# A graph layer with steps of six turns, gathers listed in pairs 20 chunks ahead, and another first part

## The chip, the cores and the metric

The kernel runs on one core of a Trainium2 chip. A core has five engines that run their own instruction lists in order and meet only through semaphores: PE (TensorE, matrix products, writes to PSUM), DVE (VectorE), ACT (ScalarE), POOL (GpSimd, which here issues the indirect DMAs) and SP (SyncE, which issues most other DMAs). The profile splits PE into PE (matmuls) and PEld (loading the stationary operand). The metric is device time in microseconds (us) of one execution; the figure given for a kernel is the median of several.

## What is computed

There are 12500 nodes with 128 features, and 400000 edges sorted by destination. Each edge carries one of two types.

```
def _L0_gnn_ref(X, edge_index, edge_types, W_data, b_data, W_control, b_control, W_self, b_self):
    src, dst = (edge_index[0], edge_index[1])
    Xs = X[src]
    m_data = Xs @ W_data.T + b_data
    m_ctrl = Xs @ W_control.T + b_control
    msg = jnp.where((edge_types == 0)[:, None], m_data, m_ctrl)
    agg = jax.ops.segment_sum(msg, dst, num_segments=X.shape[0])
    out = agg + (X @ W_self.T + b_self)
    return jax.nn.relu(out)
...
x = _layernorm(x + _L0_gnn_ref(x, edge_index, edge_type_2, ...), axis=-1)
```

Because the product with a weight is linear, the kernel sums the source rows of each destination and type first and multiplies the sums by the weights afterwards.

## The kernel before

**Tiles.** The edges form 3125 chunks of 128. A group (`g`, 25 of them) has 125 chunks and four windows (`i`); so there are 100 pairs `w = 4 g + i`, each with two windows: one of 11 or 12 chunks whose rows are fetched by indirect DMA ("gathered"), and one of 20 chunks whose rows are taken out of SBUF by one-hot matmuls ("picked"). Each row of x is held as three bf16 parts (`x3` in SBUF, `rows3` in DRAM), 384 numbers in all.

**Gathered window (`gathered`, L690 to L716).** For each chunk POOL issues one indirect DMA (L700) of 128 rows into a tile `msg`. PE then makes three matmuls with a one-hot matrix `psel` (L658) and one for the count (L712), all added up in a PSUM tile `sums`. After the last chunk DVE adds `sums` into the group's accumulator (`accumulate`, L682). The pool of `msg` has AHEAD = 24 buffers of one chunk each, and a gather stands in the program where its chunk is used. The framework's scheduler draws it forward on POOL's list as far as free buffers allow.

**Picked window (`picked`, L718 to L795).** The edges are first sorted into 100 cells of up to 32 slots by source block (`give_slots`, L505). This runs two pairs ahead, in small pieces: `before` (four matmuls, L537), `ranks` (DVE), `rank_matrix` (DVE, makes `rv`), `over`; then `put` (20 matmuls with `rv`, L601), `spread` (a copy by ACT, and two DMAs on SP: out to DRAM, L611, and back to all partitions as `pick`, L613), `turn_codes` (L621) and `keep_codes` (L631, L496, L498 on ACT, ending in `idx`). Edges beyond a cell's 32 slots go to a spare chunk that POOL gathers with `idx` (`spare_rows`, L747, tile `last`).

A picked window runs in `turns + 1` = 7 units, spread evenly over the pair:

- Units 0 to 5 each pick the rows of four cell columns: 16 matmuls (L732) into two PSUM tiles `got` (the pool `psg` has two), and two copies by ACT to `emsg` (L743).
- Units 1 to 5 also make the counts (L761) and sums (L658, with `esel`) of the unit before.
- Units 0, 1 and 3 let DVE make the one-hot `esel` (`choose`, L463). Unit 1 also issues the spare gather.
- Unit 5 carries `put` and `spread` for pair w + 2 and the last picks (`last_rows`).
- Unit 6 has no picks: it makes the sums of unit 5 and of the spare chunk, then `turn_codes` and `keep_codes`, then the addition by DVE.

**The order of the work.** `merged` sorts the units of all streams of one pair by a position between 0 and 1 and writes them out in that order: the chunks of a gathered window two pairs back (LAG = 2), the picked units, the slot pieces (0.1 to 0.75 for `begin`, 0.6 for the pick matrix), the index work of the next group (`prep_e` in the second pair of a group, `prep_p` in the third), and the parts of the finished group (`finish`). The scheduler moves instructions only where its own estimate finds an engine waiting. On each engine the list is in order, so what stands behind a waiting instruction waits too.

**The first part (L199 to L380, L903 to L918).** SP loads the first destinations of all windows into one tile `first_i`, the first groups, `near_i`. ACT issues four loads of x (L241) and then the weights (L274, L275). DVE makes tables, the windows' places (`place_i`, L372) and `near`. Then the slots of pairs 0 and 1 are made while x is split into three parts (`split_x`, L229), and `store_rows` writes the parts to DRAM. Gathers can start once they are there.

Of the kernel before, what the change touches and what calls it, by code (L numbers as in the profile page):

```python
# [46 lines left out]
AHEAD = 24  # L47
# [101 lines left out]
def short_path(ctx, tc, const, ident, eps, wT, brow, bad, x, src, dst, etype, ws, bs, out):  # L149
# [49 lines left out]
    first_i = keep.tile([1, NG, NWIN], I32, name="first_i")  # L199

    def load_first(kind):
        for i, (k, _, c, _) in enumerate(windows(0)):
            if k == kind:
                nc.sync.dma_start(
                    out=first_i[:, :, i:i + 1],
                    in_=dst.rearrange("(o g e) -> o g e", o=1, g=NG)[:, :, c * P:c * P + 1],
                )
# [65 lines left out]
    for i, (w, b) in enumerate(zip(ws, bs)):  # L273
        nc.scalar.dma_start(out=wn[:, i, :], in_=w)  # L274
        nc.scalar.dma_start(out=brow[:, i, :], in_=b.rearrange("(o d) -> o d", o=1))  # L275
# [61 lines left out]
    halves = tmp.tile([1, 2, NG * NWIN], I32, name="halves")  # L337
    nc.vector.memset(x3[:, NBLK - 1], 0.0)
    first = first_i.rearrange("o g w -> o (g w)")
    nc.vector.tensor_single_scalar(halves[:, 0, :], first, 7, op=OP.logical_shift_right)  # L340
    nc.vector.tensor_single_scalar(halves[:, 1, :], first, 127, op=OP.bitwise_and)
    halves_b = tmp.tile([1, 2, NG * NWIN], BF, name="halves_b")
    nc.vector.tensor_copy(halves_b, halves)
    fin0 = ps1.tile([P, 512], FP, name="fin")
    for i in range(2):
        nc.tensor.matmul(fin0[:, :NG * NWIN], scale[:, i, :], halves_b[:, i, :], start=(i == 0), stop=(i == 1))
    node0 = keep.tile([P, NG, NWIN], FP, name="node0")
    nc.vector.tensor_copy(node0, fin0[:, :NG * NWIN].rearrange("p (g w) -> p g w", w=NWIN))
    near = keep.tile([rows_p, NG], FP, name="near")
    from_i = tmp.tile([rows_p, 1], I32, name="from_i")  # L350
    from_f = tmp.tile([rows_p, 1], FP, name="from_f")
    nc.gpsimd.iota(from_i, pattern=[[0, 1]], base=-PAD, channel_multiplier=DPC)
    nc.vector.tensor_copy(from_f, from_i)
    for k in range(1, NE):
        ge = raw[f"ge{k}"] = tmp.tile([rows_p, 1], FP, name=f"ge{k}")
        nc.vector.tensor_scalar(
            ge, from_f, float(DPC * PB * k - PAD), float(-DPC * PB), op0=OP.is_ge, op1=OP.mult
        )
    for k in range(1, NE):
        nc.vector.tensor_add(from_f, from_f, raw.pop(f"ge{k}"))  # L360
    nc.vector.tensor_scalar(near, near_i, from_f, None, op0=OP.add)
    place = tmp.tile([1, 2, NG, NWIN], FP, name="place")
    ref = tmp.tile([1, NG, NE, 2], I32, name="ref")
    nc.gpsimd.iota(ref, pattern=[[GN, NG], [0, NE], [-PAD, 2]], base=PAD - M0, channel_multiplier=0)
    ref = ref.rearrange("o g e k -> o g (e k)")
    least = tmp.tile([1, NG, NWIN], FP, name="least")
    for i, (_, _, c, _) in enumerate(windows(0)):
        nc.vector.memset(least[:, :, i:i + 1], float(max(0, c * DPC - PAD)))
    nc.vector.tensor_tensor(place[:, 0], first_i, ref, op=OP.subtract)
    nc.vector.tensor_tensor(place[:, 1], place[:, 0], least, op=OP.max)  # L370
    nc.vector.tensor_scalar(place[:, 1], place[:, 1], float(R - WMAX), None, op0=OP.min)
    place_i = keep.tile([1, NG, NWIN], I32, name="place_i")  # L372
    nc.vector.tensor_copy(place_i, place[:, 1])
    nc.vector.tensor_tensor(place[:, 0], place[:, 0], place[:, 1], op=OP.not_equal)
    nc.vector.tensor_reduce(worst[0:1, 2, 0:1], place[:, 0].rearrange("o g w -> o (g w)"), AX.X, OP.max)

    wps = ps1.tile([P, 512], FP, name="fin")
    for i in range(3):
        nc.tensor.transpose(wps[:, i * D:(i + 1) * D], wn[:, i, :], ident)
    nc.scalar.copy(wT, wps[:, :3 * D].rearrange("p (i d) -> p i d", d=D))  # L380
# [36 lines left out]
    def prep_p(g):  # L417
# [6 lines left out]
        def first():  # L424
            nc.vector.tensor_copy(sf, s)
            nc.vector.tensor_scalar(rel, d, near[:, g:g + 1], None, op0=OP.subtract)
            codes["n", g] = code_of(rel, t, PW, 0, "p")
# [11 lines left out]
    def prep_e(g):  # L439
# [3 lines left out]
        for i in range(NE):  # L443
            cs = slice(i * EC, (i + 1) * EC)
            nc.vector.tensor_scalar(rel[:, cs], d[:, cs], node0[:, g, 2 * i + 1:2 * i + 2], None, op0=OP.subtract)
# [59 lines left out]
    def give_slots(w):  # L505
# [128 lines left out]
        s["tiled"] = {5: [put, spread], 6: [turn_codes, keep_codes]}  # L634
# [47 lines left out]
    def accumulate(g, i, ps, wide, width):  # L682

        begin_acc(g)
        with tc.issue_after(added[-2].ins) if len(added) > 1 else ExitStack():
            at = nc.vector.value_load(place_i[0:1, g, i:i + 1], min_val=0, max_val=R - WMAX)
        win = acc[g][:, :, bass.ds(at, width)]
        added.append(nc.vector.tensor_add(win, win, ps[:, :4 * wide].rearrange("p (a w) -> p a w", w=wide)[:, :, :width]))  # L688

    def gathered(g, i):  # L690
# [7 lines left out]
        def chunk(c):  # L698
            msg = mp.tile([P, 3 * D], BF, name="msg")
            nc.gpsimd.indirect_dma_start(  # L700
                out=msg, out_offset=None, in_=rows3[:, :],
                in_offset=bass.IndirectOffsetOnAxis(ap=codes["p", g][0][:, i * PB + c:i * PB + c + 1], axis=0),
            )
# [7 lines left out]
            add_rows(rows, msg, sel, c == 0, c == n - 1)  # L711
# [6 lines left out]
    def picked(w, tiled):  # L718
# [46 lines left out]

        def unit(t):

            if t < turns:
                for q in range(t * per, (t + 1) * per, pair):
                    rows(q)  # L770
            if t == 0:
                choose(0)
            if t == 1:
                choose(8)
                spare_rows()
            if t == 3:
                choose(16, 9)
            if 0 < t < turns:
                for q in range((t - 1) * per, t * per if t < turns - 1 else NQ):
                    count(q)  # L780
            if t < turns:
                for u in tiled.get(t, []):
                    u()
            if t == turns - 1:
                last_rows()
            if t > 0:
                for q in range((t - 1) * per, t * per if t < turns else NQ):
                    add_rows(cells_of(s["ps"], EW, 0), s["msg"].pop(q), s["sel"][q], False, q == NQ - 1)
            if t == turns:
                for u in tiled.get(t, []):  # L790
                    u()
                accumulate(g, 2 * i + 1, s["ps"], EW, EW)

        turns = (NQ - 1) // per
        return evenly([lambda t=t: unit(t) for t in range(turns + 1)])  # L795
# [106 lines left out]

    prep_e(0)  # L903
    merged(evenly(all_slots(0) + all_slots(1)), evenly(split_units))
# [5 lines left out]
    mp = ctx.enter_context(tc.tile_pool(name="msg", bufs=AHEAD))  # L910
# [6 lines left out]
    for u in prep_p(0):  # L917
        u()  # L918

# [8 lines left out]

    for w in range(pairs):
# [4 lines left out]
        if i == 2 and g + 1 < NG:  # L934
# [9 lines left out]
        if w + 3 < pairs:  # L944
            more += [(0.55, lambda: [u() for u in begin_slots(w + 3)])]
        merged(
            chunks.pop(w, []),
            picked(w, tiled),
# [3 lines left out]
            evenly(rest),  # L952
# [3 lines left out]
        for p in closed.pop(w, []):  # L956
# [5 lines left out]
            if gp == NG - 1 and ip in soon:  # L962
                rest += finish(gp, soon[ip])
    for u in rest:
        u()
# [158 lines left out]
```

## Time and profile before

| | us |
|---|---|
| median of 6 runs | 2384.65 |
| lowest, highest of the 6 | 2373.84, 2400.28 |
| the profiled execution | 2366.74 |
| its span | 2365.0 |
| PE busy | 1869.4 |
| DVE busy | 1583.7 |
| POOL busy | 1398.1 |
| ACT busy | 1227.6 |
| mean granted PE clock | 0.907 of full |

The page of a profile gives busy time by engine, the span in 40 slices, the DMA queues, a chain of waits followed back from the last instruction, and the costliest groups of instructions. In such a group's row the part behind the bar is busy time, the mean of one in ns, and the engine's idle time just ahead of them with what ended most of it. "Issue" is time for which no wait is seen; "remote" or "another core or an unknown queue" is a wait whose releaser is unknown. A timeline row gives start and duration in us, engine, line, operation, tiles, and in square brackets the idle time ahead of it. A matmul is pipelined and its end is modelled, so a busy PE is not PE at its peak.

The costliest groups, with the idle time ahead of them:

```profile
L700 POOL DMA_INDIRECT msg<-rows,pidx x1125 | 1280.4, 1138 | 799.7 <-PE sums L658 366.5
L743 ACT CAST emsg<-got 128x768 bf16<-128x768 f32 x1200 | 919.2, 802 | 777.3 <-PE got L732 348.5
L732 PE MATMUL got<-x,pick 128*32 128x384 bf16 x9800 | 671.4, 355 | 239.5 <-ACT emsg L743 138.5
L658 PE MATMUL sums<-esel,emsg 128*128 128x176 bf16 x7200 | 750.4, 255 | 43.3 <-issue 40.4
```

### The profile page before, as it was taken

The page shows a single profiled execution, that of the slowest core. Times are in us where ns is not written, and L with a number is a line of the kernel's source. Part 1 is how long each engine was busy: PE and PEld are TensorE (multiplying, and loading weights), DVE is VectorE, ACT ScalarE, POOL GpSimd, SP SyncE. Part 2 cuts the span into 40 slices and gives each one's busy share as a digit, 9 for nine tenths or more (in the row PEclk, how much of TensorE's full clock was granted, in tenths as well). Part 3 has the DMA queues.
Part 4 walks back from the last instruction along what each step waited for, and adds up shares of the span by engine and source line. Part 5 has one row for each costly group of instructions (what it writes and reads, how often), then busy time and mean ns, then how long its engine had stood idle before and what let it go on. Part 6 is the DMA issues. An engine that isn't in the chain of part 4 may idle for free.

```text
span 2365.0 us, 70786 instructions
## 1 busy us (share of the span) xinstructions
PE 1869.4 (79%) x28867; PEld 1369.4 (58%) x28867; DVE 1583.7 (67%) x4224; ACT 1227.6 (52%) x2322; POOL 1398.1 (59%) x1243
## 2 busy tenths in 40 slices
PE   0568778888888878887887887888887888887977
PEld 0346556665656556655665665666665566665656
DVE  6747776766666666776766776667766775676753
ACT  3435555555445555555554554545555655555645
POOL 0267675665465565665666655666665675576661
PEclk9869988998889899998899998899989998998989
DMA  7524342332333333333333333333333333333331
GB/s 205 150 80 111 94 113 76 107 101 89 101 83 107 90 100 90 109 103 88 103 88 105 109 86 102 91 100 108 94 100 102 95 98 86 106 101 107 92 94 41
DMA packets 185017, 236.73 MB, mean 100 GB/s; under 512 B 80295, under 2 KB 152282, under 8 KB 184682
## 3 DMA queue, kind: packets, MB, share of 16 engines
q0 software_dynamic: 57200, 115.59, 18.5%
q1 hardware_dynamic: 114418, 109.94, 14.9%
q10 hardware_dynamic: 13064, 6.60, 1.0%
q8 instruction: 228, 3.74, 0.7%
q14 instruction: 107, 0.88, 0.1%
HBM read 215.35 MB, written 16.64 MB: 98 GB/s over the span
## 4 chain that ended last, share of the span: by engine, by line
PE 62%; ACT 10%; issue 10%; DVE 8%; another core or an unknown queue 6%; DMA 2%; SPq 0%; DVEq 0%; ACTq 0%; POOLq 0%
PE sums L658 30%; PE got L732 22%; ACT emsg L743 8%; PE fin L850 2%; PE rk L601 2%; PE sums L761 2%; PE rk L489 1%; PE sums L712 1%; DVE esel L463 1%; DMA pick<-there 1%; PE rk L537 1%; DVE pick L643 1%; DVE rv L589 1%; ACT h L879 1%
## 5 line engine op out<-in xcount | busy, mean ns | idle before, releaser
L700 POOL DMA_INDIRECT msg<-rows,pidx x1125 | 1280.4, 1138 | 799.7 <-PE sums L658 366.5
L743 ACT CAST emsg<-got 128x768 bf16<-128x768 f32 x1200 | 919.2, 802 | 777.3 <-PE got L732 348.5
L732 PE MATMUL got<-x,pick 128*32 128x384 bf16 x9800 | 671.4, 355 | 239.5 <-ACT emsg L743 138.5
L658 PE MATMUL sums<-esel,emsg 128*128 128x176 bf16 x7200 | 750.4, 255 | 43.3 <-issue 40.4
L658 PEld LDWEIGHTS <-emsg 128*128 128x128 bf16 x7200 | 582.9, 104 | 210.6 <-issue 207.3
L463 DVE TENSOR_TENSOR esel<-code_col,code 128x1408 bf16<-128x1408 bf16 (+1 forms) x300 | 275.1, 917 | 326.7 <-PE sums L658 215.0
L732 PEld LDWEIGHTS <-pick 128*32 128x32 bf16 x9800 | 244.7, 98 | 422.5 <-issue 337.0
L658 PE MATMUL sums<-psel,msg 128*128 128x48 bf16 x3375 | 240.9, 187 | 51.2 <-issue 41.9
L658 PEld LDWEIGHTS <-msg 128*128 128x128 bf16 x3375 | 188.9, 99 | 88.3 <-issue 83.1
L747 POOL DMA_INDIRECT last<-rows,idx x100 | 113.7, 1137 | 140.1 <-DMA pdst<-in_dst_dram 92.1
L688 DVE TENSOR_TENSOR acc<-acc,sums 128x352 f32 (+1 forms) x200 | 94.1, 471 | 150.9 <-PE sums L658 46.7
L712 PE MATMUL sums<-psel,one_col 128*128 128x48 bf16 x1125 | 184.7, 186 | 11.8 <-issue 11.8
L761 PE MATMUL sums<-esel,one_col 128*32 128x176 bf16 x2500 | 168.9, 256 | 11.6 <-issue 8.1
L463 DVE TENSOR_TENSOR O<-cell_col,blk 128x2000 bf16<-128x2000 bf16 x100 | 119.3, 1193 | 45.2 <-PE got L732 22.3
L643 DVE TENSOR_SCALAR pick<-pick,lane_f 128x1600 bf16<-128x1600 bf16 x200 | 124.5, 636 | 16.4 <-DMA pick<-there 15.2
L601 PE MATMUL rk<-rv,O 128*128 128x64 bf16 x2000 | 88.2, 197 | 48.6 <-DVE rv L589 35.3
L547 DVE TENSOR_REDUCE ahead<-rk 128x100 bf16<-128x500 f32 x100 | 67.5, 675 | 83.9 <-PE got L732 56.7
L551 DVE TENSOR_TENSOR prod<-O,ahead 128x2000 bf16<-128x2000 bf16 x100 | 119.0, 1190 | 0.0
L761 PEld LDWEIGHTS <-one_col 128*32 128x32 bf16 x2500 | 85.2, 103 | 58.0 <-issue 25.5
L631 ACT CAST code<-rk 128x50 bf16<-128x50 f32 x100 | 20.1, 201 | 185.9 <-PE got L732 83.5
L712 PEld LDWEIGHTS <-one_col 128*128 128x128 bf16 x1125 | 109.7, 98 | 9.6 <-issue 9.3
L601 PEld LDWEIGHTS <-O 128*128 128x128 bf16 x2000 | 72.8, 101 | 66.1 <-issue 53.3
(170 smaller groups left out, 1992.0 us busy)
## 6 DMA issues: line engine op xcount, KB each, us to landing
pick<-there SPq DMA_DIRECT2D x100, 800.0 KB
msg<-rows,pidx POOLq DMA_INDIRECT x1125
rows<-x SPq DMA_DIRECT2D x6, 1344.0 KB
xs<-in_x_dram SPq DMA_DIRECT2D x99, 62.5 KB
out_dram<-h SPq DMA_DIRECT2D x99, 62.5 KB
xt<-in_x_dram ACTq DMA_DIRECT2D x6, 896.0 KB
psrc<-in_src_dram SPq DMA_DIRECT2D x100, 6.0 KB
pdst<-in_dst_dram SPq DMA_DIRECT2D x100, 6.0 KB
```

The lines of the kernel that those rows point to most:

```text
L463: nc.vector.tensor_tensor(sel.rearrange("p n (w t) -> p n w t", t=2), col[:rows].rearrange("p (o w t) -> p o w t", o=1, t=2).to_broadcast( ...
L551: nc.vector.tensor_tensor(prod, s["O"], ahead.rearrange("p (o j) -> p o j", o=1).to_broadcast([P, EC, NCELL]), op=OP.mult)
L601: nc.tensor.matmul(s["rk"][:m, :2 * CAP], s["held"][:, c * NCELL:c * NCELL + m], s["rv"][:, c].rearrange("p v r -> p (v r)"), start=(c == ...
L643: nc.vector.tensor_scalar(t, t, lane_f, None, op0=OP.is_equal)
L658: nc.tensor.matmul(out, msg[:, j * D:(j + 1) * D], sel, start=(start and j == 0), stop=stop, skip_group_check=True)
L688: added.append(nc.vector.tensor_add(win, win, ps[:, :4 * wide].rearrange("p (a w) -> p a w", w=wide)[:, :, :width]))
L700: nc.gpsimd.indirect_dma_start(out=msg, out_offset=None, in_=rows3[:, :], in_offset=bass.IndirectOffsetOnAxis(ap=codes["p", g][0][:, i * P ...
L712: nc.tensor.matmul(cnt, one_col, sel, start=False, stop=(c == n - 1), skip_group_check=True)
L732: nc.tensor.matmul(ps[CAP * a:CAP * (a + 1), :], slots[w]["pick"][:, a * NQ + q, :], x3[:, 4 * q + a - a0].rearrange("p j d -> p (j d)"), ...
L743: nc.scalar.copy(msg, ps[:, :, :3 * D])
L747: nc.gpsimd.indirect_dma_start(out=msg[:OVF, :], out_offset=None, in_=rows3[:, :], in_offset=bass.IndirectOffsetOnAxis(ap=slots[w]["idx"], ...
L761: nc.tensor.matmul(cells_of(s["ps"], EW, 1)[CAP * (q % 4):CAP * (q % 4 + 1), :], one_col[:, :CAP], s["sel"][q], start=(q < 4), stop=(q + 4 ...
```

## The change

No arithmetic is changed. Four things are.

1. **Joined steps.** A pair has six units instead of seven. What was unit 6 becomes `end`, which `picked` hands back; it is run inside unit 0 of the next pair, behind that unit's picks and its `choose`. After the last pair it runs by itself. The spare gather moves from unit 1 to unit 2. The parts of a finished group start at 0.1 of the pair instead of 0.
2. **Placing one unit earlier.** `put` and `spread` stand in unit 4 of 6 instead of unit 5 of 7.
3. **Gathers listed ahead.** A tile `msg` holds SB = 2 chunks, and the pool has HOLD = 12 such tiles. `fetch` issues the gathers of one tile. Ten tiles (AHEAD = 10, 20 chunks) are fetched before the loop, and one more each time a chunk with an even number is used. `prep_p` moves to the second pair of a group.
4. **First part.** `first_i` becomes two tiles, `first_e` and `first_p`, and `node0` is made from `first_e` alone. The weights and biases are loaded on SP's queue instead of ACT's. One unit of the split of x stands ahead of `prep_e(0)`. The places, `near` and the turned weights become `places_and_weights`, at 0.97 of the merged first work (the scheduler still draws its small DVE operations forward).

The core of the diff:

```diff
-AHEAD = 24
+SB = 2
+HOLD = 12
+AHEAD = 10
...
-    first_i = keep.tile([1, NG, NWIN], I32, name="first_i")
+    first_i = {k: keep.tile([1, NG, NE], I32, name=f"first_{k}") for k in "ep"}
...
-        nc.scalar.dma_start(out=wn[:, i, :], in_=w)
-        nc.scalar.dma_start(out=brow[:, i, :], in_=b.rearrange("(o d) -> o d", o=1))
+        nc.sync.dma_start(out=wn[:, i, :], in_=w)
+        nc.sync.dma_start(out=brow[:, i, :], in_=b.rearrange("(o d) -> o d", o=1))
...
-        s["tiled"] = {5: [put, spread], 6: [turn_codes, keep_codes]}
+        s["tiled"] = {4: [put, spread], 6: [turn_codes, keep_codes]}
...
+    to_fetch = [(g, i, c) for g in range(NG) for i in range(NE) for c in range(0, PC[i], SB)]
+    fetched = []
+
+    def fetch():
+        if to_fetch:
+            g, i, c = to_fetch.pop(0)
+            msg = mp.tile([P, SB, 3 * D], BF, name="msg")
+            for k in range(min(SB, PC[i] - c)):
+                at = i * PB + c + k
+                nc.gpsimd.indirect_dma_start(
+                    out=msg[:, k, :], out_offset=None, in_=rows3[:, :],
+                    in_offset=bass.IndirectOffsetOnAxis(ap=codes["p", g][0][:, at:at + 1], axis=0),
+                )
+            fetched.append(msg)
...
-            msg = mp.tile([P, 3 * D], BF, name="msg")
-            nc.gpsimd.indirect_dma_start(
...
-            )
+            if c % SB == 0:
+                fetch()
+                s["msg"] = fetched.pop(0)
...
-            add_rows(rows, msg, sel, c == 0, c == n - 1)
+            add_rows(rows, s["msg"][:, c % SB, :], sel, c == 0, c == n - 1)
...
-    def picked(w, tiled):
+    def picked(w, tiled, ending):
...
+        def add(q0, q1):
+            for q in range(q0, q1):
+                add_rows(cells_of(s["ps"], EW, 0), s["msg"].pop(q), s["sel"][q], False, q == NQ - 1)
+
         def unit(t):
 
-            if t < turns:
-                for q in range(t * per, (t + 1) * per, pair):
-                    rows(q)
+            for q in range(t * per, (t + 1) * per, pair):
+                rows(q)
+            if t in (0, 1):
+                choose(8 * t)
             if t == 0:
-                choose(0)
-            if t == 1:
-                choose(8)
+                ending()
+            if t == 2:
                 spare_rows()
...
-            if t == turns:
-                for u in tiled.get(t, []):
-                    u()
-                accumulate(g, 2 * i + 1, s["ps"], EW, EW)
+                add((t - 1) * per, t * per)
+
+        def end():
+
+            add((turns - 1) * per, NQ)
+            for u in tiled.get(turns, []):
+                u()
+            accumulate(g, 2 * i + 1, s["ps"], EW, EW)
 
         turns = (NQ - 1) // per
-        return evenly([lambda t=t: unit(t) for t in range(turns + 1)])
+        return evenly([lambda t=t: unit(t) for t in range(turns)]), end
...
+    split_units.pop(0)()
     prep_e(0)
-    merged(evenly(all_slots(0) + all_slots(1)), evenly(split_units))
+    merged([(0.97, places_and_weights)], evenly(all_slots(0) + all_slots(1)), evenly(split_units))
...
+    for _ in range(AHEAD):
+        fetch()
...
-        if i == 2 and g + 1 < NG:
+        if i == 1 and g + 1 < NG:
             more += evenly(prep_p(g + 1), 0.1, 0.7)
...
+        units, ending = picked(w, tiled, ending)
         merged(
             chunks.pop(w, []),
-            picked(w, tiled),
+            units,
...
-            evenly(rest),
+            evenly(rest, 0.1),
         )
...
+    ending()
```

## The prediction

> **What bounds the kernel now.** I read the page's totals and chain of waits first, then the waits of PE between 225 and 2325 us (the steady part: 92 of the 100 pairs of windows), then the timeline around one pair's end, then POOL's timeline.
>
> ```profile
> PE 1869.4 (79%) x28867; PEld 1369.4 (58%) x28867; DVE 1583.7 (67%) x4224; ACT 1227.6 (52%) x2322; POOL 1398.1 (59%) x1243
> ...
> PE 62%; ACT 10%; issue 10%; DVE 8%; another core or an unknown queue 6%; DMA 2%; SPq 0%; DVEq 0%; ACTq 0%; POOLq 0%
> ```
>
> No engine is full. PE leads the chain, but a fifth of it is ACT and time for which the profile names no cause. The starts of the pairs' last rows (L658 with `last`) stand 22.75 us apart on average. An undisturbed step (16 picks at L732, 4 counts, 12 sums, two chunks) took 2.05 us, from 1199.76 to 1201.81, so a pair with six full steps needs some 15 us of PE. The rest is waiting, and matmuls stretched by waits.
>
> ```profile
> PE got L732 <- ACT emsg L743: 113.7, 163, 4.7
> PE got L732 <- issue: 84.8, 146, 2.8
> PE sums L658 <- issue: 74.3, 170, 1.7
> PE rk L537 <- ACT part L498: 16.9, 27, 1.2
> ```
>
> These are PE's own waits in that stretch: total us, times, longest. Two kinds hold nearly all: picks that wait until ACT has copied the rows out of `got`, and waits without a releaser. PE idles 377 us there in all. I sorted the gaps by how many groups of 16 picks the pair had behind it: 81 us fall behind its first group, 132 behind the second, and 15, 41, 44, 17 and 45 in the other places. The ACT waits are 26.1 us behind the first and 52.2 behind the second. The loss sits where one pair ends and the next begins. The timeline shows why (start, duration, engine, line):
>
> ```profile
> 1214.85 0.47 ACT L756 CAST last<-got 64x384 bf16<-64x384 f32 x1
> 1215.58 1.07 PE L658 MATMUL sums<-esel,emsg 128*128 128x176 bf16 x12
> 1217.45 0.83 PE L732 MATMUL got<-x,pick 128*32 128x384 bf16 x16
> 1218.71 0.20 ACT L631 CAST code<-rk 128x50 bf16<-128x50 f32 x1 [3.38 <-PE sums L658]
> 1218.94 1.50 ACT L743 CAST emsg<-got 128x768 bf16<-128x768 f32 x2
> 1219.79 0.51 PE L732 MATMUL got<-x,pick 128*32 128x384 bf16 x8 [0.20 <-ACT emsg L743]
> ```
>
> The old last step (sums alone) gives ACT nothing to copy: it idles 3.38 us. The old first step (picks alone) fills both `got` buffers and leaves PE little to do while they are copied, so the second step's picks wait.
>
> The third reading is POOL. Here is PE in four stretches of one pair (length; busy of PE, PEld, DVE, ACT, POOL; granted clock):
>
> ```profile
> 1200.00:1202.60 2.60, 2.60 (x60) 1.88 (x52) 1.79 (x4) 1.50 (x2) 2.09 (x2) 1.00 0.22 57
> 1202.60:1206.00 3.40, 2.00 (x28) 1.32 (x20) 2.99 (x8) 0.00 (x0) 2.49 (x4) 1.00 0.28 74
> 1206.00:1209.80 3.80, 1.72 (x15) 0.54 (x18) 1.59 (x5) 1.67 (x4) 2.44 (x3) 0.86 0.24 66
> 1209.80:1213.00 3.20, 3.20 (x44) 2.41 (x46) 0.50 (x1) 1.71 (x4) 1.57 (x3) 0.63 0.25 67
> ```
>
> From 1202.6 PE trickles, though its matmuls wait for nothing that is named. Through it POOL issues gathers without a break:
>
> ```profile
> 1201.70 0.95 POOL L700 DMA_INDIRECT msg<-rows,pidx  x1 [0.30 <-issue]
> 1202.95 0.95 POOL L700 DMA_INDIRECT msg<-rows,pidx  x1 [0.30 <-issue]
> 1204.20 0.95 POOL L700 DMA_INDIRECT msg<-rows,pidx  x1 [0.30 <-issue]
> ```
>
> Over the steady part, with runs broken by a pause of 0.5 us, PE idles 8% of the time in which a gather is first or second of its run (78 of 979 us) and 33% from the third on (217 of 667 us, 463 gathers, some five a pair). That is 0.35 us a late gather (1.44 us by 0.245). At the start a run of 24, from 101 to 132 us, holds PE, ACT and DVE almost still. Only the coincidence is seen; the cause is not. The Trainium skill (Runtime: NRT & Kernel Launch, Instruction fetch mechanics) offers another suspect only to clear it: the fetch of the next block of instructions is called mostly hidden. The 228 fetches of 16 KB on the instruction queue bear that out so far, at 0.7% of the DMA engines' time; by that rule nothing in the sum changes.
>
> **The change part by part.**
>
> *First part.* The halves need only the four early first values; the split of x stands ahead, and the weights go from ACT's queue to SP's. ACT's first copy of x stood at 26.02 us, behind weight issues that ended at 23.27. Its own load was issued by 12.54. DVE's first subtraction (28.39) now stands directly behind the cast of `psrc`, which ran at 22.98 when its load had landed, so it can gain at most 5 us. On SP six weight issues move ahead of the row stores, and the nine bias issues that took 31.98 to 37.65 move behind the sixth store: even. The last two row stores still follow all bias parts. Ends -5 and +5; I take -3.
>
> *First gathers.* Twenty gathers now stand ahead of the first two spare gathers (L747): 20 by 1.25 us. The first spare issue goes from 96.8 to about 122. Behind it waits the first pair's end on PE, now inside pair 1's first step, and everything behind that on PE. Before, pair 1 crept through the same run and ended at 141.4. Now five steps and an end remain from about 124, at 3 us each: 142. Ends -5 and +8; I take 0.
>
> *Joined steps.* Seven steps become six: the end (12 sums, 3 of `last`, 4 and 7 small ones, the addition on DVE) goes behind the next pair's 16 picks. These picks' two copies (1.50 us) now run beside 15 sums (1.07 for 12, 0.39 for 3) and the small ones (0.20 and 0.39), about 2 us. The ACT waits behind the first two groups (26.1 and 52.2) should go: -78. No instruction is added. A wait is worsened: L537 of the next ranks needs the copies of the codes (L631, L496, L498, 0.2 us each at most, plus the hand-over), and it now follows the end with only two chunks and one pick between (16 picks before). If it waits 0.45 us in all pairs that is 44 us instead of 16.9. The other 15 picks of the second step stand behind it, then ACT's copies of these. I add 12. Ends: all 113.7 us of ACT waits gone; or none gone and the 27 added. Value -66. DVE's addition after the end stands ahead of the ranks' reduction, and `sums` waited 9.1 us on it all told; the pairs' fewer free moments of that buffer cost at most as much again, inside these ends.
>
> *Placing one step earlier.* The middle of step 5 of 7 is 0.786 of a pair, of step 4 of 6 it is 0.75: 0.8 us sooner. It needs `rv`, done at 1206.77 where PE placed at 1213.47; that 6.7 us hides it, and without it the price would be 0.8 us a pair, 78 us. SP issues the same two DMAs. Zero. The earlier index work of the next group is a handful of operations under 0.3 us on a DVE that is 33% free: zero; without that cover some 2 us a group, 50 us.
>
> *Gathers by twos.* Same number, 1138 ns each, depth still about 23. The second of a tile never waits for PE, so runs of one vanish; against that, PE's clump of four or five chunks around a pair's end is spread to about two a step. The spare gather moves one step later and still joins a run. The listing keeps 11 or 12 gathers between spares. POOL needs 15.6 us a pair (12.5 by 1.25) whatever the order. Ends: no third places left, -164 (463 by 0.35); every gather a late one, +240 (680 by 0.35). These two tendencies pull apart, so I take 0, nearest to the present rows.
>
> *Clock.* The granted clock is about 0.91 in the steady part, so roughly 156 of 1731 busy us are stretch, and the low stretch in the windows above (0.63) follows the trickle. Idle falls by 66 of 377 us; in proportion that is -28. Ends -28 and 0; I take -14. The Trainium skill (TensorE: Matmul & The Clock Gate, What's actually happening) speaks against it: half rate comes after an idle window of about 3.4 us. The waits removed average 0.7 us (113.7 by 163), too short to trip that, and by the rule this term would be 0 and the sum 14 us smaller.
>
> Sum: -3, 0, -66, 0, 0, -14: -83. From the profiled span, 2365.0, that is 2282, with the 1.7 us around it 2284. The median of the six runs lies 17.9 us above that execution (2366.7), so I expect 2302.
>
> **The rivals.**
>
> *A, the forecast: 0.49.* 2302; its own range, with half of the terms' ends, 2255 to 2350.
>
> *B, runs of gathers break up too: 0.15.* For it: two chunks a step is less than POOL's pace, so it could pause after each tile. Against it: a shorter pair leaves POOL fewer pauses. With two thirds of the 164 us: 2302 - 110 = 2192.
>
> *C, the waits only change their name: 0.12.* PE stops at L537, or at the second step, for what it saved, or the trickle fills the place. For it: the waits without a releaser sit in the same places as the ACT waits. Time 2385, give or take 12.
>
> *D, slower, by longer runs of gathers: 0.24.* Place: a tile's two gathers, the spare one and the next tile's two, in the third step. A run of five puts three in late places where POOL comes in late; since 3.75 us of gathers meet a step of 3.5, it does not recover and the next tile joins. From two more late gathers a pair (69 us) it cancels the joined steps. At four more, 138 us against 83: about 2440. For it: POOL's 15.6 us in a pair of 21 instead of 22.75 leaves fewer pauses. Against it: in 453.8 us it waited for PE, and that slack does not vanish.
>
> **How the numbers follow.** The predicted time is A's. B's lower half and most of D lie outside 2195 to 2405, no more than 0.2 in all. What a measurement here can tell from no change is about 0.5%, 12 us. Faster: A nearly whole, B, a little of C: 0.66. Same: most of C: 0.10. Slower: D: 0.24.
>
> **What would show it.** Right: PE's wait for ACT at the picks falls from 113.7 to under 50 us; ACT's long wait ahead of the codes (L631) shrinks; L537's wait is at most doubled; the pair's period is 21.9 us; pair 1 still ends near 142. Wrong: waits without a releaser grow by more than the ACT waits shrink; PE idles much more or less than 217 us beside third and later gathers; the period is the same while the start moves by 20 us.

## The result, and the profile after

The changed kernel took 2382.19 us (median of 36 runs, 2368.38 to 2394.23), the kernel before 2384.3 us in the runs beside it (78 runs). The ratio is 0.9998, 95% interval 0.9982 to 1.0014: no difference that can be measured, where 2302 us was forecast. The profiled span went from 2365.0 to 2369.3 us, at a granted clock of 0.915 instead of 0.907.

The page of the changed kernel (totals, chain of waits, costliest groups; in a group's row busy time and mean ns stand behind the first bar, idle time ahead of it and what ended most of it behind the second):

```profile
PE 1861.8 (79%) x28867; PEld 1356.5 (57%) x28867; DVE 1569.7 (66%) x4225; ACT 1228.4 (52%) x2322; POOL 1470.2 (62%) x1243
...
PE 63%; issue 10%; ACT 9%; DVE 7%; another core or an unknown queue 7%; DMA 1%; POOL 1%; DVEq 0%; ACTq 0%; SPq 0%; POOLq 0%
...
L707 POOL DMA_INDIRECT msg<-rows,pidx x1125 | 1347.8, 1198 | 815.1 <-PE sums L665 248.4
L765 ACT CAST emsg<-got 128x768 bf16<-128x768 f32 x1200 | 921.6, 802 | 728.7 <-PE got L754 418.8
L754 PE MATMUL got<-x,pick 128*32 128x384 bf16 x9800 | 699.2, 349 | 198.6 <-ACT emsg L765 119.4
L665 PE MATMUL sums<-esel,emsg 128*128 128x176 bf16 x7200 | 746.6, 253 | 24.2 <-issue 22.5
```

The shares of the chain hardly moved. PE's own waits from 225 to 2325 us (total us, times, longest):

```profile
PE got L754 <- ACT emsg L765: 110.8, 131, 7.8
PE got L754 <- issue: 60.0, 111, 3.7
PE rk L544 <- ACT part L505: 52.7, 36, 4.4
PE sums L665 <- issue: 40.6, 109, 1.5
```

The wait that was to fall from 113.7 to under 50 us is 110.8. The rank matmuls (L544, L537 before) wait 52.7 us for ACT's `part` instead of 16.9. Waits without a releaser shrank. In all PE idles 371 us in this stretch and 369 before (2100 less the busy 1729.41 and 1731.36 us of the two profiles).

By the starts of the 100 pairs' last rows, pairs 5 to 99 took 22.70 us each (22.63 before). The fifth of these starts stands at 197.4 us instead of 205.3, and what follows the 99th took 38.0 us instead of 32.0. So 7.9 us were gained in the first part, and 6.2 lost in the pairs and 6.0 behind them. From here on "a pair" is this time between the fifth and the 99th start, divided by 94.

### The profile page after: what moved, and what is told of

Read it like the earlier page. It is cut to its first block, busy times and chain, and to the rows that moved or that the text cites. A ratio compares the mean times of both kernels' runs of the same rounds, so it can differ in the third digit from the quotient of the medians.

```text
span 2369.3 us, 70186 instructions
## 1 busy us (share of the span) xinstructions
PE 1861.8 (79%) x28867; PEld 1356.5 (57%) x28867; DVE 1569.7 (66%) x4225; ACT 1228.4 (52%) x2322; POOL 1470.2 (62%) x1243
## 4 chain that ended last, share of the span: by engine, by line
PE 63%; issue 10%; ACT 9%; DVE 7%; another core or an unknown queue 7%; DMA 1%; POOL 1%; DVEq 0%; ACTq 0%; SPq 0%; POOLq 0%
PE sums L665 27%; PE got L754 23%; ACT emsg L765 6%; PE fin L877 3%; PE rk L608 3%; PE sums L783 2%; PE rk L544 1%; PE sums L733 1%; PE rk L496 1%; DVE esel L470 1%; POOL msg L707 1%; DMA msg<-rows,pidx 1%; ACT h L906 1%; ACT last L778 0%
## 5 line engine op out<-in xcount | busy, mean ns | idle before, releaser
L707 POOL DMA_INDIRECT msg<-rows,pidx x1125 | 1347.8, 1198 | 815.1 <-PE sums L665 248.4
L754 PE MATMUL got<-x,pick 128*32 128x384 bf16 x9800 | 699.2, 349 | 198.6 <-ACT emsg L765 119.4
L665 PE MATMUL sums<-esel,emsg 128*128 128x176 bf16 x7200 | 746.6, 253 | 24.2 <-issue 22.5
L665 PEld LDWEIGHTS <-emsg 128*128 128x128 bf16 x7200 | 570.5, 103 | 209.8 <-issue 194.1
L695 DVE TENSOR_TENSOR acc<-acc,sums 128x352 f32 (+2 forms) x200 | 94.1, 470 | 372.1 <-PE sums L665 191.2
L665 PE MATMUL sums<-psel,msg 128*128 128x48 bf16 x3375 | 225.8, 187 | 33.6 <-issue 22.4
L783 PE MATMUL sums<-esel,one_col 128*32 128x176 bf16 x2500 | 181.7, 249 | 23.7 <-issue 19.1
L733 PE MATMUL sums<-psel,one_col 128*128 128x48 bf16 x1125 | 177.2, 186 | 14.6 <-issue 14.6
L783 PEld LDWEIGHTS <-one_col 128*32 128x32 bf16 x2500 | 91.4, 100 | 69.3 <-issue 44.3
L544 PE MATMUL rk<-prod,ltri 128*128 128x125 bf16 x400 | 44.0, 237 | 80.0 <-ACT part L505 62.1
```

Source lines behind the costliest of these rows:

```text
L665: nc.tensor.matmul(out, msg[:, j * D:(j + 1) * D], sel, start=(start and j == 0), stop=stop, skip_group_check=True)
L707: nc.gpsimd.indirect_dma_start(out=msg[:, k, :], out_offset=None, in_=rows3[:, :], in_offset=bass.IndirectOffsetOnAxis(ap=codes["p", g][0] ...
L733: nc.tensor.matmul(cnt, one_col, sel, start=False, stop=(c == n - 1), skip_group_check=True)
L754: nc.tensor.matmul(ps[CAP * a:CAP * (a + 1), :], slots[w]["pick"][:, a * NQ + q, :], x3[:, 4 * q + a - a0].rearrange("p j d -> p (j d)"), ...
L783: nc.tensor.matmul(cells_of(s["ps"], EW, 1)[CAP * (q % 4):CAP * (q % 4 + 1), :], one_col[:, :CAP], s["sel"][q], start=(q < 4), stop=(q + 4 ...
```

## The experiments

There were six series, each beside the kernel before on one chip. The kernel before took 1981, 2426, 1974, 2432, 2430 and 2383 us in them, though it was the same program, and the third and fourth series are listed under the same chip. So there are two levels, "1980" and "2400". The first record belongs to the second. A ratio is always to the kernel before of the same series.

| what was run | at 1980 | at 2400 |
|---|---|---|
| joined steps alone | 1.0405 (1.0371 to 1.0439); 1.0315 (1.0273 to 1.0357) | 0.9804 (0.9757 to 0.9851) |
| listing by twos alone | 1.0089 (1.0054 to 1.0124) | |
| first part alone | | 0.9952 (0.9918 to 0.9985) |
| the whole change | | 0.9963 (0.9942 to 0.9983); 0.9946 (0.9912 to 0.9980) |
| the change without the listing | | 0.9812 (0.9760 to 0.9864) |
| the change with tiles of one chunk | | 0.9787 (0.9737 to 0.9837); 0.9864 (0.9828 to 0.9901) |
| before, half the gathers | 0.8941 (0.8911 to 0.8971); 0.8925 (0.8891 to 0.8959) | 0.7663 (0.7616 to 0.7709) |
| the change, half the gathers | 0.9120 (0.9089 to 0.9150); 0.9157 (0.9123 to 0.9192) | 0.7718 (0.7675 to 0.7762) |
| the change, POOL slowed by writes | 1.2155 (1.2117 to 1.2194) | |

**First series (1980): the parts, and half the gathers.** The first run takes over `picked` with `end`, `ending`, the later start of a finished group's parts and the earlier placing, nothing else. The second takes over `fetch` and the earlier `prep_p` alone:

```diff
 # joined steps alone, on the kernel before
-    def picked(w, tiled):
+    def picked(w, tiled, ending):
...
 # listing alone, on the kernel before
+    for _ in range(AHEAD):
+        fetch()
```

> The kernel before with the joined steps and the earlier placing alone; gathers and first part as before. Theory 1 (gathers pay back): PE is held by POOL's runs of gathers, so a turn without stops only brings PE sooner to where POOL is; ratio to the kernel before within 0.995 to 1.005, and PE's idle time beside the third and later gathers of a run stays near the 217 us of before. Theory 2 (the waits only move): ratio within 0.995 to 1.005 too, but with about 110 us of waits for ACT's emsg in other places of the pair. Theory 3 (the listing by twos gave the gain back): ratio 0.965 to 0.98, as forecast for the joined steps.

> The kernel before with the gathers listed 20 ahead by twos alone; steps and first part as before. Theory 1 and theory 2: within 0.995 to 1.01. Theory 3: ratio 1.02 to 1.035, the loss that hides the joined steps' gain, with more runs of eight and longer on POOL.

The other two leave out every second chunk's gather in either kernel, so that 600 of 1125 are left (in the kernel before there are then 12 row tiles instead of 24):

```diff
 # the changed kernel; in the kernel before, `if c % 2 == 0:` ahead of the gather
-            for k in range(min(SB, PC[i] - c)):
+            for k in range(1):
...
-            add_rows(rows, s["msg"][:, c % SB, :], sel, c == 0, c == n - 1)
+            add_rows(rows, s["msg"][:, 0, :], sel, c == 0, c == n - 1)
```

> The kernel before with every second chunk's gather left out; PE uses the row tile of the chunk before it in its place, so PE, DVE and ACT do the same work. The sums are of the wrong rows. Theory 1: PE's idle time of 217 us beside the third and later gathers shrinks to under 80, the waits of 114 us for ACT's emsg behind the pair's end stay; 2200 to 2260 us, ratio 0.925 to 0.95. If gathers don't slow PE: ratio above 0.985.

> The changed kernel with every second chunk's gather left out in the same way (the second chunk of a tile uses the rows of the first). The sums are of the wrong rows. Theory 1: with the gathers no longer the pace the joined steps are worth what was forecast for them; 50 to 80 us less than the kernel before with half its gathers. Theory 2: the same as the kernel before with half its gathers, within 15 us, since the waits for ACT only move. Theory 3: 50 to 80 us less, as theory 1, which the run of the joined steps alone tells from it.

Measured: 1.0405, 1.0089, 0.8941 and 0.9120. None of the theories had the joined steps lose. The listing alone stayed where theories 1 and 2 had it. Half the gathers were worth more than expected, and the changed kernel with half its gathers lies 35 us above the other one, not 50 to 80 below it. Why the joined steps lose at this level shows in two rows of their page, POOL's gathers and PE's sums of the spare chunk:

```profile
L700 POOL DMA_INDIRECT msg<-rows,pidx x1125 | 1439.4, 1280 | 342.9 <-issue 156.4
...
L658 PE MATMUL sums<-esel,last 128*128 128x176 bf16 x300 | 45.2, 267 | 194.2 <-DMA last<-rows,idx 194.2
```

From 225 to 1700 us POOL never pauses for half a microsecond: its list of gathers sets the pace, and the spare gather, now one step later, comes late in it. PE loses 194 us there. The row of picks in the kernel with the listing alone, which has the seven steps of before, is as telling:

```profile
L747 PE MATMUL got<-x,pick 128*32 128x384 bf16 x9800 | 593.1, 345 | 17.2 <-ACT emsg L758 10.5
```

With the old order of steps PE waits 10.5 us for ACT here, where the first record has 138.5 in the same row. The kernel before with half its gathers, which also has the old order, waits 11.0 us. The order of the steps alone makes no such wait.

**Second series (2426): the same kernels again, and the first part.** The kernel before itself, the changed kernel itself, and the kernel before with the new first part (`first_i` split, weights on SP, `places_and_weights`).

> The kernel before itself, for a profile beside the other runs. Theory 1 (PE, ACT and DVE are slowed beside POOL's long runs of gathers, as in the profile first shown): about 2365 us with PE idle for 30 to 45% of the time beside the third and later gathers of a run. If instead the runs of this series go as the first experiments went: about 1980 us, POOL issuing gathers nearly without a pause, and PE idle for under 5% of the time beside them.

> The changed kernel itself. Theory 1: the gain of the joined steps is there only where the gathers do not slow PE; beside a kernel before of 2384 us the ratio is 1.000, beside one of 1980 us 0.96 to 0.98. Rival from the first experiments: where POOL's gathers are the pace, the joined steps alone lost 4% and the listing by twos alone 1%, and both together give 0.99 to 1.04, whatever the waits for ACT do.

> The kernel before with the new first part alone; steps and gathers as before. All theories: the first pair's end moves forward by 3 to 8 us and the pairs after it go on as before, ratio 0.995 to 1.0. If POOL's gathers are the pace, an earlier first gather (2 us in the profiles) is all that is gained: ratio 0.998 to 1.0.

The kernel before took 2416.9 us in the execution that was profiled, the changed kernel gave 0.9963, the first part alone 0.9952 (12 us, 4 to 20). In the kernel before PE again idled for about a third of the time beside the third and later gathers of a run (36%; 33% in the first record). What differs from the first series shows in the timeline of the kernel before (start, duration, engine, line, operation, tiles; in brackets idle time and its releaser):

```profile
1237.17 0.83 PE L732 MATMUL got<-x,pick 128*32 128x384 bf16 x16
...
1237.88 0.16 ACT L498 COPY part<-rk 64x2 f32<-64x2 f32 x1
...
1238.10 0.40 PE L537 MATMUL rk<-prod,ltri 128*128 128x125 bf16 x4
...
1239.35 1.17 POOL L747 DMA_INDIRECT last<-rows,idx  x1 [0.30 <-issue]
...
1241.43 0.80 ACT L743 CAST emsg<-got 128x768 bf16<-128x768 f32 x1 [3.39 <-remote]
1241.60 0.68 DVE L547 TENSOR_REDUCE ahead<-rk 128x100 bf16<-128x500 f32 x1 [1.22 <-remote]
```

The 16 picks are done by 1238.0, ACT is free at 1238.04, and the copy of these picks starts at 1241.43. PE's next picks wait for that copy. I counted this over all 1200 copies of a run: a copy is late if it starts more than 0.2 us after both its eighth pick's end (as modelled) and ACT's instruction before it. At 1980 two to six copies are late, 0.7 to 2.1 us in all, in each of the eight profiles of the first and third series. At 2400 it is 346 copies and 535 us in the first record before, 308 and 418 us after, 336 and 581 us in this series' kernel before. No copy had to wait for a free `emsg` buffer: with the last reader of its buffer counted in, the sums stay the same. And ACT is not alone. DVE's reduction in the last row needs the rank matmuls, which end at 1238.50, and starts at 1241.60, though DVE is free from 1240.37. Counted in the same way, 64 of the 100 such reductions are late in this profile, 79 us in all, and none in the kernel with the listing alone at 1980. So what comes late is PE's results, as far as the modelled ends of matmuls can tell; if the matmuls in truth ended later than the profile puts them, it would look the same.

**Third series (1974): by chance at the other level again.** The joined steps and the half gathers were repeated as they stood, and one kernel slows POOL:

```diff
             msg = mp.tile([P, SB, 3 * D], BF, name="msg")
+            nc.gpsimd.memset(msg, 0.0)
```

> The kernel before with the joined steps and the earlier placing alone, once more, since the kernel before took 1981 us beside the first experiments and 2426 beside the next. Theory 1 (PE, ACT and DVE are slowed while POOL lists gathers in an unbroken run; a turn without stops brings PE sooner to such a run), where the kernel before takes about 2400: ratio 0.99 to 1.01, the waits for ACT's emsg stay over 90 us. Theory 3 (the listing by twos gave the gain back): 0.965 to 0.98. Where the kernel before takes about 1980: 1.04 again, PE waiting for the spare gather.

> The kernel before with every second chunk's gather left out (the sums are of the wrong rows). Theory 1, where the kernel before takes about 2400: PE's idle time of about 220 us beside the third and later gathers of a run falls to under 100, the ratio to 0.89 to 0.93. If the gathers are not what slows PE there: above 0.97.

> The changed kernel with every second chunk's gather left out (the sums are of the wrong rows). Theory 1, where the kernel before takes about 2400: with fewer gathers the joined steps are worth 50 to 80 us, so that much below the kernel before with half its gathers. Theory 2 (the stop at the end of a pair only changes its place, to L544's wait for ACT's part and to the last picks): within 25 us of it. Where the kernel before takes about 1980: 1.02 times it, as before.

> The changed kernel with a write of zeros by POOL to each row tile ahead of its two gathers (the gathers then fill it), so that no run of gathers is longer than two or four without a pause. Theory 1, where the kernel before takes about 2400: PE's idle time beside third and later gathers (214 us) shrinks to under 80 while POOL stays under its own floor of some 19 us a pair; ratio 0.93 to 0.97. If the length of a run is only where PE happens to be late, and not what slows it: 1.0 to 1.03. Where the kernel before takes about 1980, POOL has no time for pauses: 1.03 to 1.1.

The first three repeat the first series: 1.0315, 0.8925, 0.9157. The fourth, 1.2155, is above its range. Rows of its page (totals, the writes, the spare chunk's sums):

```profile
PE 1806.2 (75%) x28867; PEld 1340.6 (56%) x28867; DVE 1673.4 (70%) x4225; ACT 1224.8 (51%) x2322; POOL 1940.5 (81%) x1843
...
L705 POOL MEMSET msg<- 128x768 bf16 x600 | 450.3, 757 | 63.9 <-DMA pick<-there 63.0
...
L665 PE MATMUL sums<-esel,last 128*128 128x176 bf16 x300 | 52.8, 301 | 439.5 <-DMA last<-rows,idx 439.5
```

POOL's list grew by 450 us, and the kernel stands 428 us above the kernel before (2402.0 less 1974.4; the changed kernel itself was not run at this level): here POOL's list is the bound. Whether pauses help at 2400 was not seen.

**Fourth series (2432): the test that was wanted.**

> The changed kernel itself, in one call with the next three. Where the kernel before takes about 2400: 0.995 to 1.0. Where it takes about 1980: PE has no late starts of ACT to make up, POOL's gathers are the pace in both, and the joined steps' loss (1.03 to 1.04, PE waiting for the spare gather) and the listing's (1.01) meet: if they add up 1.04 to 1.05, if the listing ahead keeps the spare gather from waiting behind the others 1.0 to 1.01.

> The kernel before with every second chunk's gather left out (the sums are of the wrong rows). Where the kernel before takes about 2400: if ACT's late starts belong to the gathers, half of them go, and the ratio falls to 0.86 to 0.92; if they have another cause it stays above 0.97. Where the kernel before takes about 1980: 0.893.

> The changed kernel with every second chunk's gather left out (the sums are of the wrong rows). Where the kernel before takes about 2400: 50 to 80 us below the kernel before with half its gathers if the gathers' late starts swallow the gain; within 25 us of it, or above it, if the waits only moved. Where the kernel before takes about 1980: 0.914.

> The kernel before with the joined steps and the earlier placing alone. Where the kernel before takes about 2400: 0.965 to 0.98 if the listing by twos gave the gain back, 0.995 to 1.01 if the gain was never there. Where it takes about 1980: 1.03 to 1.04.

Measured: the change 0.9946, half the gathers 0.7663 and 0.7718, the joined steps alone 0.9804. The last says that the gain was there, 48 us (36 to 59), and that the rest of the change took it back: in this series the changed kernel stands 31.8 us above the joined steps alone (2419.11 to 2387.28). Theory 1 (within 1%) and the plain form of theory 2 fall; the value lies at the upper end of theory 3's range (0.965 to 0.98).

Half the gathers are worth 566 us at this level (2431.99 to 1866.47), 1.08 us for each of the 525 left out, against 0.40 us at 1980 (211 by 525). The 0.7663 lies far below the 0.86 to 0.92 that were expected if the late starts belong to the gathers. The late starts fall to 145 copies, 147 us. But the two halved kernels hardly tell what the joined steps are worth, as I had meant them to: without these gathers PE and DVE are both close to full,

```profile
PE 1648.2 (88%) x28867; PEld 1259.1 (67%) x28867; DVE 1564.7 (84%) x4224; ACT 1221.9 (65%) x2322; POOL 912.9 (49%) x718
```

and theory 1's "50 to 80 us below" met 11 us above.

The waits of PE in the joined steps alone, 225 to 2325 us:

```profile
PE got L733 <- ACT emsg L744: 104.0, 121, 6.4
PE got L733 <- issue: 70.5, 122, 3.1
PE rk L537 <- ACT part L498: 63.2, 44, 5.1
PE sums L658 <- issue: 49.4, 104, 1.2
```

The waits for `emsg` and `part` are 167 us here, 130.6 in the first record before and 163.5 after; in the second series they are 148.4 before and 168.9 after. The kernel that gains 48 us has more of them than either profile of the kernel before, and as many as the changed kernel.

**Fifth series (2430): which half of the listing costs.** One run gives the changed kernel the gathers of before (24 single tiles, each gather where its chunk is used); the other keeps the listing and changes the tile:

```diff
-SB = 2
-HOLD = 12
-AHEAD = 10
+SB = 1
+HOLD = 24
+AHEAD = 20
```

> The changed kernel with the gathers as in the kernel before (24 tiles of one chunk, each gather where its chunk is used). Where the kernel before takes about 2430 us: 0.970 to 0.980 if the listing gives the gain back (0.980 for the joined steps times 0.995 for the first part is 0.976), faster than both kernels; 0.990 to 1.0 if the gains of the parts do not add up and the listing is not to blame. Where it takes about 1980: 1.02 to 1.04, since the spare gather then waits behind the others.

> The changed kernel with tiles of one chunk (24 of them), still listed 20 chunks ahead. Where the kernel before takes about 2430 us: 0.970 to 0.982 if the tile of two chunks, freed as one, is what costs; 0.990 to 1.0 if it is the listing ahead. Where it takes about 1980: within 0.01 of the changed kernel, whose ratio there is not yet measured, about 1.0 to 1.02.

0.9812 and 0.9787: both below either kernel's ratio, and equal within their intervals (the first lies just above its range of 0.970 to 0.980, the second in its own). Listing 20 chunks ahead costs nothing that can be measured; the tile of two chunks costs. The changed kernel was not run in this series, so its ratio comes from the fourth. Against the 0.9946 of the changed kernel that is 0.0159 of 2430 us, 39 us (24 to 53, with the halves of the two intervals added in quadrature). Where they go shows when the same 94 pairs are cut out of the two profiles (length; busy of PE, PEld, DVE, ACT, POOL; clock). The changed kernel in the fourth series:

```profile
194.40:2375.20 2180.80, 1774.32 (x27202) 1290.44 (x27200) 1423.12 (x3807) 1126.98 (x2154) 1392.72 (x1168) 0.91 0.32 95
```

With tiles of one chunk:

```profile
205.10:2342.60 2137.50, 1759.35 (x27200) 1286.88 (x27198) 1419.63 (x3807) 1131.19 (x2152) 1406.52 (x1159) 0.91 0.32 96
```

The same work at the same clock takes 43.3 us longer (28.1 with the changed kernel's profile of the second series, 23.04 us a pair). Two thirds is idle time of PE, a third matmuls that are stretched. The idle time has no clear place. In these stretches PE waits 0 us for a gather's rows to land (5.6 us with tiles of one). The largest difference is L544's wait for ACT's `part`, 65.7 against 46.2 us, but the other kernel of this series, with single tiles too, has 58.2 us of it between 225 and 2325 us. PE's idle time beside third and later gathers is 228 us in both. The start goes the other way: the fifth pair of the changed kernel begins 10.7 us sooner (1.5 in the second series). Behind the pairs it takes 38.0 us against 30.8. There the trace shows POOL's last drain: 9.7 us in all five profiles with full tiles of two, 0.7 us in every one with tiles of one and all gathers, 1.4 to 1.5 in both kinds where half the gathers are left out.

**Sixth series (2383): the rank matmuls later.** On the kernel with tiles of one:

```diff
-            (0.1, before), (0.2, ranks), (0.24, lambda: s["spares"][1]()), (0.3, rank_matrix), (0.75, over),
+            (0.2, before), (0.26, ranks), (0.3, lambda: s["spares"][1]()), (0.35, rank_matrix), (0.75, over),
```

> The changed kernel with tiles of one chunk and the rank matmuls at 0.2 of a pair instead of 0.1 (ranks at 0.26, their matrix at 0.35), so that ACT's part is done when PE comes to L544. If that stop is a price of its own: the 46 us of waits for ACT's part go to under 10, and the ratio is 0.955 to 0.97 where the kernel before takes about 2430 us. If PE is held up wherever it is early, as theory 2 has it: the wait turns up at another place (the picks behind ACT's emsg over 140 us in all) and the ratio is within 0.005 of 0.979. Where the kernel before takes about 1980: no difference to the same kernel with the ranks at 0.1, about 1.0 to 1.02.

The edit did not reach PE. Behind the first step's picks and the end of the last pair, L544 still has only one pick ahead of it in over half of the pairs and nine or ten in a quarter, as without the edit (in the kernel before, all 16 of the first step's picks stand between the end and it): the scheduler draws it forward. Its wait is 53.6 us. So the question that the run was meant for stays open, and it counts as a repeat of the tiles of one: 0.9864 on a chip whose kernel before takes 2383 us, as in the first record, where the changed kernel had 0.9998. That puts the price of the tile of two at 32 us (22 to 41) there. Its 2352.22 us are the lowest time at this level.

## Why the prediction was wrong, by its own steps

**Gathers by twos: the step that failed.** It took 0 between -164 and +240, since "these two tendencies pull apart". By undoing the tile alone it costs 39 us where the kernel before takes 2430, and 32 where it takes 2383. The two tendencies don't cancel. About 7 us are POOL's last drain, which the prediction did not have at all, and 28 to 43 are longer pairs, less 1.5 to 10.7 us at the start. That the tile costs is shown; by which path is open. A tile is free only when both its chunks are used, so POOL may get its buffers later, but then PE should wait for rows, and the profile names no such wait. Windows of 11 chunks also leave half a tile empty (24 tiles for 45 chunks), so that 12 tiles hold 22.5 chunks on average and not 24. No run separates these.

**Joined steps: -66 forecast, -48 measured (36 to 59), and for another reason.** The steps without stops were worth some three quarters of the size, but the picks' wait for ACT did not go: 104.0 us in the joined steps alone, forecast under 50 (113.7 in the first record before, 128.0 in the second series). The reading behind it, that a sums-only step followed by a picks-only step makes PE wait for ACT, is contradicted by the 10.5 us of the same row at 1980, with the same seven steps. At 2400 ACT starts a quarter to a third of its copies late. In the kernel before nearly half of this time falls on the second step (275 of the 581 us of the second series); in the joined steps alone they are spread over all six (59 to 110 us each). The prediction's own timeline has such a late start in it. The copy of the codes (L631) needs these matmuls:

```profile
1216.80 0.20 PE L621 MATMUL rk<-ident_b,cell 128*32 128x25 bf16 x4
```

They end at 1217.00, and the copy starts at 1218.71. The median of this hand-over is 0.92 us in this profile and 0.35 us in the listing alone at 1980. So half of the 3.38 us that were put down to a lack of work was a wait for a result that the profile shows as done. In the joined steps alone the late starts come to 478 us, against 581 in the kernel before (second series). That the gain is this difference is not shown, and one figure speaks against it: the changed kernel has fewer still, 436 and 440 us in the second and fourth series, without the gain.

**L537's wait: put at 44 us instead of 16.9, with 12 of it in the sum; it came to 52.7 in the changed kernel and 63.2 in the joined steps alone.** I had placed it behind two chunks and one pick and priced the small copies at 0.45 us. The place was right. The copies ahead of it on ACT are subject to late starts too (longest 5.1 us). Rival C named this place, and its time came true, but not its mechanism: the kernel with the joined steps alone has the longer wait and the gain.

**First part: -3 forecast.** Alone -12 (4 to 20); on top of the joined steps nothing that can be measured (0.9812 against 0.9804). The fifth pair's start came 7.9 us earlier in the first record, but it goes partly with the tiles of two: 194.4 to 203.5 us in the three profiles of the changed kernel, 205.1 to 209.8 in the three that have the first part with joined steps and single tiles. **First gathers: 0.** Pair 1 ended at 132.2, not 142, with PE waiting 22.0 us for the first spare gather.

**Placing: 0.** No run of its own; it is in the 48 us of the joined steps. **Clock: -14.** It was to follow from idle time that did not go (369 us before, 371 after; the prediction's 377 is 8 more than its own 1731 busy us leave). The granted clock went from 0.907 to 0.915 all the same, and PE's busy time a pair from 18.67 to 18.63 us. The mean wait of 0.7 us could not rule the term out either: its row has waits of up to 4.7 us. That the clock can give more is seen where gathers are left out: 0.99, and 16.4 us of PE a pair instead of 18.8 (kernel before, fourth and second series).

**Rival D** had the direction of the twos right, with runs of gathers as mechanism. There are more such gathers, but PE's idle time beside third and later ones is 214 us (217 before), so it isn't that.

Together, at 2430: -48 for the joined steps, 0 to -12 for the first part, +39 for the twos: -9 to -21, measured -9 and -13 in two series and -0.5 in the first record.

## What to carry to other kernels

A wait that a profile names can be the place where a general delay surfaces: before pricing its removal, look whether the releaser had long been done when the wait ended. Price a buffer that is freed in larger pieces on its own, and take it apart from a change of order that it comes with; here three constants kept the order and restored the gain. And change a unit's position only with a look at where the scheduler puts its instructions.

## What the runs showed of the hardware

The same program took 1974 to 1981 us in two series and 2383 to 2432 in the others. At the upper level ACT starts copies up to 15 us after PE's picks have ended by the profile, 535 to 581 us in a run of the kernel before, and at the lower 0.7 to 2.1 us. DVE's reductions behind PE are late at the upper level too. It is not the gathers' transfers as such: from the end of a gather's issue to its last packet the median is 1.4 us both in the first record before and in the kernel with the listing alone at the lower level. Nor is it the fetch of instructions: 105 of the 346 late starts of the first record overlap one, and 84 to 117 would if the same stretches lay 5 to 20 us earlier or later. With half the gathers the late starts fall to 147 us, so most of them go with the gathers; but at the lower level, in the joined steps and in the listing alone, POOL issues gathers without a pause and hardly a copy is late, so gathers alone don't make them. What makes one level or the other, and why PE's results are seen late, stays open.
